# Two-layer adaLN transformer on one core: rows and sorts of the last experts given out earlier, their gathers made riders, their sums a part later

## The chip, the cores and the metric

The kernel runs on one core of one Trainium2 chip. The metric is the device time of one launch in microseconds (us), the median of several runs. Besides it there is one profiled execution; its trace gives every instruction's start and length on the engines: PE (TensorE matmul), PEld (TensorE weight load), DVE (VectorE), ACT (ScalarE), POOL (GpSimd) and SP (SyncE, which only issues DMAs here).

## The reference

Two transformer layers on x of shape (4, 1024, 256), all in float32. Each layer adds a gated attention and then a gated mixture of experts; c gives shift, scale and gate of each by a small product.

```python
h = _layernorm(x) * (1 + ca) + sa
x = x + ga * _L0_attn_ref(h, ...)      # causal softmax attention, 16 heads
h = _layernorm(x) * (1 + cb) + sb
x = x + gb * _L0_ffn_ref(h, ...)       # 16 experts, two products with GELU, best 2 of 16 per row
h = _layernorm(x) * (1 + ca) + sa      # second layer, its own c and weights
x = x + ga * _L1_attn_ref(h, ...)      # linear attention: cubed, normalised q and k
h = _layernorm(x) * (1 + cb) + sb
x = x + gb * _L1_ffn_ref(h, ...)       # the last experts, below

def _L1_ffn_ref(x, router_w, router_b, expert_w, expert_b):   # 8 experts, E = 8
    probs = jax.nn.softmax(xt @ router_w + router_b, axis=-1)
    gate, idx = jnp.max(probs, axis=-1), jnp.argmax(probs, axis=-1)
    out_all = jnp.einsum('th,ehd->ted', xt, expert_w) + expert_b[None, :, :]
    return gate[:, None] * jnp.take_along_axis(out_all, idx[:, None, None], axis=1)[:, 0, :]
```

So each of the 4096 rows goes to one of the eight last experts, the one with the largest router value.

## The kernel before, in words

x of the four batches stays in SBUF (`k.x[b]`, 128 rows x 8 tiles x 256). Four stages follow one another: attention 0, experts 0, attention 1, experts 1; the tail of each overlaps the head of the next. The change concerns the last two.

**Who sets the order.** The program text emits instructions; the tile framework reorders what does not depend on each other, except that instructions given to `k.pin` keep their order of emission on their engine. Each engine then runs its own queue in order. Text from different stages is interleaved by `Around`: a list of *tasks* (generators that are stepped one after the other, each `yield` worth some pieces) and a list of *riders* (generators of DMAs; only the first in the list is stepped). `around.step(pieces, rides)` advances both; the loop of attention 1 and that of the last experts call it at every step. An indirect DMA (`scatter`, `gather`) waits in addition for `k.anchor`, the matmul emitted last before it, so that these DMAs are spread over the stage.

**Attention 1** (`attention1`) runs over five rounds b = 0 to 4: `front(b)` (layer norm, transposes `ps_lnT` L153, products `ps_k` L1511, `ps_kv` L1502, `ps_q` L1537) beside `back(b - 1)` (`ps_o` L1574 with `on` L1580 on VectorE, transposes `ps_oT` L1589, a convolution along the rows into `y` L1597 and L1601, the projection `ps_pr` L1609, added to x at L1614). One step is taken of each in turn, and `pace[b] / 6` pieces of the tasks with each round of steps. When both are finished, `after_batch(b - 1)` gives out the tasks for the experts of that batch:

- `rows(b)`: layer norm statistics of the new x, then `routed_rows`: in two halves q of four tiles, `h` (L1030 on ScalarE; for batches 0 and 1 scaled and shifted by VectorE at L1045 and L1046) is stored to DRAM as `rows_in` (L1048), transposed (`ps_lnT` L1057) to `hT` (L1063, L1068), multiplied with the router (`ps_route` L794), turned (L799) and turned back (`ps_logits` L802).
- `sort(p)` for each of the three parts `PARTS = ((0, 1), (2,), (3,))` of batches: softmax, then the place of each row in an order by expert: two products `ps_rank` (L895), a chain of small VectorE operations, `index` (L933) and `ps_expert` (L949) with `offset` (L950). At its end it adds the rider `send(p)`, which reads the rows (`hs<-rows_in`, L1870) and scatters them (L964) to DRAM, sorted by expert.

**The last experts** (`Experts1.run`) work on tiles of 128 sorted rows, in 25 pairs of tiles: 11 of part 0, 7 of part 1, 7 of part 2. A pair: `xs<-sorted` (L1008, loads run up to five pairs ahead), transposes `ps_xT` (L1923) to `xT` (ScalarE, L1927 or L1930), and one pair later the product `ps_y` (L1938) with the expert's weights, found at a column that TensorE and VectorE load into a register from `offset` (L955); VectorE adds the bias (L1944) and for parts 1 and 2 multiplies the gate (L1946), and SP stores the pair (`results<-y`, L1947). While part p is not sent, the loop steps the tasks and riders; after each pair it takes `step(2, 2)`.

After a part's last pair comes the task `combine(p)`: for each of its row tiles a gather `ys<-results` (L974, issued by POOL, four ahead of its use, six buffers) and then a weighting by the router's probability: for part 0 `out` on ScalarE (L2002), gate and sum on VectorE (L2007, L2008), for parts 1 and 2 one VectorE operation (L1996). Every four tiles `out_dram<-x` is stored (L2010). After part 1, `count_sums` counts sums within bounds (12 VectorE operations, L495 to L498); after part 2, `out_of_bounds` turns the counts into a flag on which a general version of the whole, not run here, is taken or left.

Of the kernel before, what the change touches and what calls it, by code (L numbers as in the profile page):

```python
# [8 lines left out]
F32 = mybir.dt.float32  # L9
I32 = mybir.dt.int32  # L10
AF = mybir.ActivationFunctionType
ALU = mybir.AluOpType
# [479 lines left out]
def count_within(k, good, recs, low, high, count):  # L492

    nc = k.nc
    k.pin(nc.vector.tensor_scalar(good, recs, low, None, ALU.is_ge))  # L495
    nc.vector.tensor_scalar(recs, recs, high, None, ALU.is_le)
    nc.vector.tensor_tensor(good, good, recs, ALU.mult)
    nc.vector.tensor_reduce(count, good, AX.X, ALU.add)  # L498


def count_sums(k, pool):

    recs = [k.recs.rearrange("p n i j -> p (n i j)")]
    recs += [k.recs1[:, i].rearrange("p b t h -> p (b t h)") for i in range(2)]
    inverse = 1.0 / SUM_HI, 1.0 / SUM_LO
    for i, (rec, (low, high)) in enumerate(zip(recs, (inverse, (SUM_LO, SUM_HI), inverse))):
        good = pool.tile([P, 8 * B * H], F32, tag="xs", name="good", bufs=6)
        count_within(k, good, rec, low, high, k.good[:, i : i + 1])


def out_of_bounds(k, pool, psum):
# [505 lines left out]
def routed_rows(k, work, b, statistics, scale, shift, wr, br, ne, logits, scalar):  # L1017
# [31 lines left out]
        return h  # L1049

    h = yield from normalised(0)
    for q in range(2):
        hT = work.tile([P, CC, 512], F32, tag="hT", name="hT", bufs=1)
        for cc in range(CC):
            ps = k.misc.tile([P, 512], F32, tag="m", name="ps_lnT")
            for i in range(4):
                tr = nc.tensor.transpose(  # L1057
                    ps[:, i * P : (i + 1) * P], h[:, i, cc * P : (cc + 1) * P], k.ident
                )
                if i == 0:  # L1060
                    k.pin(tr)
            if scale is None:
                nc.scalar.activation(  # L1063
                    hT[:, cc], ps, AF.Identity,
                    bias=k.modF[:, cc, b : b + 1], scale=k.modF[:, 2 + cc, b : b + 1],
                )
            else:
                nc.scalar.copy(hT[:, cc], ps)  # L1068
            if q == 0 and cc == CC - 1:
                h = yield from normalised(1)  # L1070
            else:
                yield 1
        yield from route_logits(k, hT, wr, br, ne, work, logits[:, 4 * q : 4 * q + 4])
# [371 lines left out]
def attention1(ctx, k, a, after_batch=lambda b: None):  # L1445
# [172 lines left out]
    for b in range(B + 1):  # L1618
        while b == HB and k.awaited in k.around.tasks:
            k.around.step()  # L1620
        todo = ([front(b)] if b < B else []) + ([back(b - 1)] if b else [])
        pace = (6, 8, 6, 6, 12)[b]
        n = 0
        while todo:
            todo = [g for g in todo if next(g, k) is not k]
            n += pace
            k.around.step(n // 6)
            n %= 6
        if b:
            after_batch(b - 1)  # L1630


def attention1_general(ctx, k, a):
# [150 lines left out]
class Experts1:  # L1784


    def __init__(self, k, a, out):
# [16 lines left out]
        whole = Sorting(k, rt, E1, 1, NT * len(PARTS[0]))  # L1804
        fewer = whole.of_fewer(rt, NT)
        self.sortings = [whole if len(p) > 1 else fewer for p in PARTS]
        self.sent = set()

    def load_weights(self):
        k, a, nc = self.k, self.a, self.k.nc  # L1810
# [52 lines left out]
    def send(self, p, index):  # L1863
# [16 lines left out]
                yield  # L1880
        self.sent.add(p)

    def run(self, early):

        k = self.k
        nc = k.nc
        work = self.back = self.stack.enter_context(
            k.tc.tile_pool(name="f1_work", bufs=2, reuse_waits="tile")
        )
        ps_x = self.stack.enter_context(  # L1890
            k.tc.tile_pool(name="f1_ps_x", bufs=4, space=PSUM, reuse_waits="tile")
        )
        ps_o = self.stack.enter_context(
            k.tc.tile_pool(name="f1_ps_o", bufs=4, space=PSUM, reuse_waits="tile")
        )
        k.misc = ps_x

        pairs = [
            (p, list(range(g, min(g + 2, s.tiles))))
            for p, s in enumerate(self.sortings)  # L1900
            for g in range(0, s.tiles, 2)
        ]
        coming = []

        def fetch(n):

            for p, tiles in pairs[n + len(coming) : n + 5]:
                if p not in self.sent:
                    break
                xs = work.tile([P, 2, C], F32, tag="xs", name="xs", bufs=6)  # L1910
                k.sorted1[p].load(xs[:, : len(tiles)], tiles)
                coming.append(xs)

        def tiles_of(p, tiles, xs):

            n = len(tiles)
            at = self.sortings[p].offsets(
                self.state[p][1], tiles, [mybir.EngineType.PE, mybir.EngineType.DVE]
            )
            ps = ps_x.tile([P, 2, CC, P], F32, tag="m", name="ps_xT")  # L1920
            for j in range(n):
                for cc in range(CC):
                    nc.tensor.transpose(ps[:, j, cc], xs[:, j, cc * P : (cc + 1) * P], k.ident)  # L1923
            xT = work.tile([P, 2, CC, P], F32, tag="xT", name="xT", bufs=3)
            b = PARTS[p][0] if len(PARTS[p]) == 1 else None
            if b is None:
                nc.scalar.copy(xT[:, :n], ps[:, :n])  # L1927
            else:
                for cc in range(CC):
                    nc.scalar.activation(  # L1930
                        xT[:, :n, cc], ps[:, :n, cc], AF.Identity,
                        bias=k.modF[:, cc, b : b + 1], scale=k.modF[:, 2 + cc, b : b + 1],
                    )
            yield
            po = ps_o.tile([P, 2, C], F32, tag="o", name="ps_y")
            for j in range(n):
                for cc in range(CC):
                    k.anchor = nc.tensor.matmul(  # L1938
                        po[:, j], lhsT=xT[:, j, cc], rhs=self.we[:, cc, bass.ds(at[j], C)],
                        start=cc == 0, stop=cc == CC - 1,  # L1940
                    ).ins
            y = work.tile([P, 2, C], F32, tag="y", name="y", bufs=3)
            for j in range(n):
                nc.vector.tensor_tensor(y[:, j], po[:, j], self.be[:, bass.ds(at[j], C)], ALU.add)  # L1944
            if b is not None:
                nc.vector.tensor_tensor(y[:, :n], y[:, :n], bcast(self.gate[:, b], 1, n), ALU.mult)  # L1946
            nc.sync.dma_start(k.results1[p].part(tiles), y[:, :n])  # L1947

        again, before = None, None
        for n, (p, tiles) in enumerate(pairs):  # L1950
            if p not in self.sent and before is not None:
                next(before, None)
                before = None
            while p not in self.sent:
                k.around.step(1, 2)
            fetch(n)
            now = tiles_of(p, tiles, coming.pop(0))
            next(now)
            if before is not None:
                next(before, None)  # L1960
            before = now
            if n + 1 == len(pairs) or pairs[n + 1][0] != p:
                next(before, None)
                before = None
                if early and p + 2 == len(PARTS):
                    count_sums(k, work)
                if early and p + 1 == len(PARTS):
                    again = out_of_bounds(k, work, ps_x)
                k.around.tasks.append(self.combine(p))
            k.around.step(2, 2)  # L1970
        k.around.drain()
        self.stack.close()
        return again

    def combine(self, p):
        k, work = self.k, self.back
        nc = k.nc
        index, _, part = self.state[p]
        most = self.sortings[p].nt

        def fetch(n):
            ys = work.tile([P, C], F32, tag="ys", name="ys", bufs=6)
            self.sortings[p].gather(ys, k.results1[p], index[:, 0, n : n + 1])
            return ys

        coming = []
        for n in range(4):
            coming.append(fetch(n))
            yield 0.5
        for n in range(most):  # L1990
            j = n % 2
            b, t = PARTS[p][n // NT], n % NT
            ys = coming.pop(0)
            if len(PARTS[p]) == 1:
                xs = k.x[b][:, t]
                k.pin(nc.vector.scalar_tensor_tensor(  # L1996
# [2 lines left out]
            else:  # L1999
                if j == 0:  # L2000
                    y = work.tile([P, 2, C], F32, tag="out", name="out")
                k.pin(nc.scalar.activation(y[:, j], ys, AF.Identity, scale=part[:, n : n + 1]))  # L2002
            if n + 4 < most:
                coming.append(fetch(n + 4))
            if j == 1 and len(PARTS[p]) > 1:
                xs = k.x[b][:, t - 1 : t + 1]
                nc.vector.tensor_tensor(y, y, bcast(self.gate[:, b], 1, 2), ALU.mult)  # L2007
                nc.vector.tensor_tensor(xs, xs, y, ALU.add)  # L2008
            if t % 4 == 3:
                nc.sync.dma_start(  # L2010
# [176 lines left out]
```

## Time and profile before

| | us |
|---|---|
| median of 3 runs (lowest, highest) | 1087.03 (1085.85, 1088.48) |
| the profiled execution | 1087.63 |
| its span in the trace | 1085.8 |
| last `ps_pr` of attention 1 ends | 969.5 |
| last `ps_y` of the last experts ends | 1059.7 |
| last `y` of the last experts ends | 1062.15 |
| gathers (L974) of part 0, 1, 2 are issued at | 1010.8 to 1033.0, 1039.2 to 1050.3, 1065.1 to 1075.3 |

The span begins with the first instruction of the trace. A row of a window or group gives busy time; a wait is put down to the instruction that released the engine. A matmul in float32 appears twice in the trace's counts. Times from the trace are starts plus lengths, and two neighbouring instructions of an engine can overlap by some 0.1.

### The profile page before, as it was taken

The page shows a single profiled execution, that of the slowest core. Times are in us where ns is not written, and L with a number is a line of the kernel's source. Part 1 is how long each engine was busy: PE and PEld are TensorE (multiplying, and loading weights), DVE is VectorE, ACT ScalarE, POOL GpSimd, SP SyncE. Part 2 cuts the span into 40 slices and gives each one's busy share as a digit, 9 for nine tenths or more (in the row PEclk, how much of TensorE's full clock was granted, in tenths as well). Part 3 has the DMA queues.
Part 4 walks back from the last instruction along what each step waited for, and adds up shares of the span by engine and source line. Part 5 has one row for each costly group of instructions (what it writes and reads, how often), then busy time and mean ns, then how long its engine had stood idle before and what let it go on. Part 6 is the DMA issues. An engine that isn't in the chain of part 4 may idle for free.

```text
span 1085.8 us, 18090 instructions
## 1 busy us (share of the span) xinstructions
PE 945.7 (87%) x6072; PEld 559.8 (52%) x6072; DVE 620.4 (57%) x1987; ACT 602.5 (55%) x959; POOL 336.0 (31%) x528
## 2 busy tenths in 40 slices
PE   4899999999999999889679989986997989858760
PEld 2434434443443434335568878874464656547550
DVE  5822235422465155413676767993899968564572
ACT  0368655765477555775555657766654745523430
POOL 2013211311232234663004615612550100553632
PEclk9999999999999999999899999998999899989875
DMA  6995000100010001552825556624223201458764
GB/s 206 358 346 179 1 1 6 40 1 1 1 64 1 1 30 54 201 215 78 317 88 170 197 177 189 196 75 144 67 65 148 88 2 39 141 170 264 240 205 130
DMA packets 97142, 132.89 MB, mean 122 GB/s; under 512 B 8536, under 2 KB 84216, under 8 KB 96528
## 3 DMA queue, kind: packets, MB, share of 16 engines
q1 hardware_dynamic: 84656, 97.27, 26.9%
q0 software_dynamic: 11776, 33.57, 9.9%
q8 instruction: 52, 0.85, 0.3%
q10 hardware_dynamic: 608, 0.79, 0.3%
q14 instruction: 50, 0.41, 0.1%
HBM read 67.85 MB, written 63.75 MB: 121 GB/s over the span
## 4 chain that ended last, share of the span: by engine, by line
PE 63%; DVE 19%; issue 5%; DMA 5%; ACT 4%; POOL 1%; SPq 1%; DVEq 0%; ACTq 0%; POOLq 0%
PE ps_s L388 13%; PE ps_av L453 12%; PE ps_qk L364 6%; PE ps_y L1312 5%; PE ps_h L1247 4%; PE ps_v L349 3%; PE ps_out L427 3%; PE ps_pr L1609 3%; PE ps_y L1938 3%; PE ps_q L1537 2%; PE ps_k L1511 2%; DVE y L1601 2%; DMA ys<-results,index 2%; PE ps_lnT L1057 1%; DVE st L1258 1%
## 5 line engine op out<-in xcount | busy, mean ns | idle before, releaser
L396 ACT ACTIVATE pT<-ps_s 128x1024 f32<-128x1024 f32 x288 | 279.3, 1022 | 169.7 <-PE ps_s L388 167.2
L399 POOL TENSOR_SCALAR_AFFINE_SELECT pT<-pT 128x256 f32<-128x256 f32 x256 | 104.2, 431 | 328.4 <-ACT pT L396 323.7
L388 PE MATMUL ps_s<-qT,kT 32*128 32x512 f32 (+3 forms) x1536 | 178.8, 523 | 0.1
L453 PE MATMUL ps_av<-pT,v 128*32 128x512 f32 (+3 forms) x1536 | 165.2, 497 | 9.4 <-DVE turned L411 5.6
L964 POOL DMA_INDIRECT sorted<-hs,index x96 | 96.2, 1002 | 144.9 <-PE ps_y L1312 73.0
L974 POOL DMA_INDIRECT ys<-results,index x96 | 102.7, 1070 | 119.0 <-DMA results<-y 43.6
L388 PEld LDWEIGHTS ps_s<-qT,kT 32*128 32x128 f32 x1536 | 74.5, 185 | 95.5 <-issue 72.8
L453 PEld LDWEIGHTS ps_av<-pT,v 128*32 128x32 f32 x1536 | 40.6, 108 | 104.0 <-issue 58.7
L1247 PE MATMUL ps_h<-w,xT 128*128 x352 | 82.1, 386 | 6.5 <-DVE mv L1259 3.8
L1312 PE MATMUL ps_y<-w,act 128*128 x352 | 83.7, 392 | 4.2 <-DVE rs_seed L84 2.8
L411 DVE STREAM_TRANSPOSE turned<-ps_av 128x512 f32<-128x512 f32 x32 | 22.8, 712 | 98.9 <-PE ps_av L453 98.6
L1312 PEld LDWEIGHTS ps_y<-w,act 128*128 128x128 f32 x352 | 67.7, 197 | 14.0 <-ACT act L1295 4.8
L1247 PEld LDWEIGHTS ps_h<-w,xT 128*128 128x128 f32 x352 | 66.2, 193 | 15.9 <-issue 4.2
L1295 ACT ACTIVATE act<-ps_hT,gain 128x128 f32<-128x128 f32 x176 | 63.6, 463 | 16.9 <-PE ps_hT L1286 16.8
L1270 ACT ACTIVATE hid<-hid,nmr,rstd 128x256 f32<-128x256 f32 x88 | 47.5, 603 | 39.4 <-DVE nmr L1263 39.2
L1511 PE MATMUL ps_k<-wqkv,hT 128*128 128x512 f32 x128 | 61.9, 603 | 3.6 <-DMA wqkv<-in_wqkv_dram 2.8
L1938 PE MATMUL ps_y<-we,xT 128*128 x200 | 53.0, 412 | 10.6 <-ACT xT L1930 8.4
L371 DVE COPY qT<-ps_qk 128x512 f32<-128x512 f32 x16 | 11.0, 688 | 81.8 <-PE ps_qk L364 81.8
L103 DVE BATCH_NORM_STATS2 ln_st<-x 128x6 f32<-128x256 f32 x128 | 49.2, 407 | 0.5
L1255 DVE TENSOR_TENSOR hid<-ps_h,b 128x256 f32<-128x256 f32 x88 | 33.9, 415 | 26.6 <-PE ps_h L1247 21.5
L1938 PEld LDWEIGHTS ps_y<-we,xT 128*128 128x128 f32 x200 | 38.2, 204 | 20.1 <-ACT xT L1930 11.6
L374 DVE TENSOR_SCALAR kT<-ps_qk,par 128x512 f32<-128x512 f32 x32 | 22.5, 745 | 37.0 <-PE ps_qk L364 37.0
(223 smaller groups left out, 1499.4 us busy)
## 6 DMA issues: line engine op xcount, KB each, us to landing
xs<-sorted SPq DMA_DIRECT2D x69, 256.0 KB, 3.8
results<-y SPq DMA_DIRECT2D x69, 256.0 KB, 3.0
sorted<-zero SPq DMA_DIRECT2D x2, 6016.0 KB, 20.1
rows_in<-h SPq DMA_DIRECT2D x16, 512.0 KB, 2.9
hs<-rows_in POOLq DMA_DIRECT2D x32, 256.0 KB, 3.5
w<-in_w_dram SPq DMA_DIRECT2D x8, 1024.0 KB, 11.3
x<-in_x_dram SPq DMA_DIRECT2D x4, 1024.0 KB, 6.5
b<-in_b_dram SPq DMA_DIRECT2D x2, 2048.0 KB
```

Of the source, the lines that this page charges most:

```text
L364: nc.tensor.matmul(ps, lhsT=w[:, cc, g * P : (g + 1) * P], rhs=hT[:, cc, hf * 512 : (hf + 1) * 512], start=cc == 0, stop=cc == CC - 1,)
L388: k.anchor = nc.tensor.matmul(pair[hh // 2][:, hh % 2, c0 : c0 + w], lhsT=kTs[o][rows, kb * P : (kb + 1) * P], rhs=qT[rows, q1 - w : q1], ...
L396: nc.scalar.activation(pT, ps, AF.Exp, scale=1.0 / L**0.5)
L399: nc.gpsimd.affine_select(out=pT[:, :, c0 : c0 + P], in_=pT[:, :, c0 : c0 + P], compare_op=ALU.is_ge, fill=0.0, base=0, pattern=[[0, 2], [ ...
L453: nc.tensor.matmul(po[32 * hh : 32 * hh + 32, 512 - w :], lhsT=vs[b % 2][:, kb, 8 * g + 2 * hh + o, :], rhs=exps[b, g, o, u][hh // 2][:, h ...
L964: i = self.k.nc.gpsimd.indirect_dma_start(out=buffer.ap, out_offset=bass.IndirectOffsetOnAxis(ap=index, axis=0), in_=rows, in_offset=None, ...
L974: self.paced(self.k.nc.gpsimd.indirect_dma_start(out=rows, out_offset=None, in_=buffer.ap, in_offset=bass.IndirectOffsetOnAxis(ap=index, a ...
L1247: mm = nc.tensor.matmul(ph[:, j], lhsT=xTs[i // 2][:, j, cc], rhs=w1[:, cc, bass.ds(at[i + j], C)], start=cc == 0, stop=cc == CC - 1,)
L1295: o = nc.scalar.activation(act[:, j, cc], pt[:, j, cc], AF.Gelu, bias=gain[:, 1, cc, t : t + 1], scale=gain[:, 0, cc, t : t + 1],)
L1312: mm = nc.tensor.matmul(po[:, j], lhsT=acts[i // 2][:, j, cc], rhs=w2[:, cc, bass.ds(at[i + j], C)], start=cc == 0, stop=cc == CC - 1,)
L1511: k.anchor = nc.tensor.matmul(ps, lhsT=hT[:, cc, t * P : (t + 1) * P], rhs=wqkv[:, cc, C:], start=cc == 0, stop=cc == CC - 1,).ins
L1938: k.anchor = nc.tensor.matmul(po[:, j], lhsT=xT[:, j, cc], rhs=self.we[:, cc, bass.ds(at[j], C)], start=cc == 0, stop=cc == CC - 1,).ins
```

## The change

Five edits, all in attention 1 and the last experts:

1. `after_batch(b - 1)` is called as soon as `back(b - 1)` has ended, while `front(b)` still runs; the pace of round 3 goes from 6 to 8, and rounds 3 and 4 step two riders, not one.
2. For batches 2 and 3 (no scale given) both halves of `h` are made and stored ahead of the first transpose.
3. Gathers become riders of their own (`gathers(p)`), given out at a part's end; all 32 have 24 buffers. The sums come later: `combine(0)` is given out after part 1, `combine(1)` and `combine(2)` after the last pair. They no longer gather, but take what lies in `got`.
4. `count_sums` yields after each of its three arrays; one is counted after each of the pairs 7, 8 and 9 of part 0.
5. The step after a pair is 4 pieces, not 2, until the last part is sent. Transposes, `xT` and first products of a pair, and the gate of `combine`, are pinned.

The body of a pair moves from local functions to methods (`fetch`, `tiles_of`, `pair`, `products`) and is otherwise the same.

```diff
@@ routed_rows
     h = yield from normalised(0)
+    second = (yield from normalised(1)) if scale is None else None
...
             if q == 0 and cc == CC - 1:
-                h = yield from normalised(1)
+                if second is None:
+                    h = yield from normalised(1)
+                else:
+                    h = second
+                    yield 1
@@ attention1
-        todo = ([front(b)] if b < B else []) + ([back(b - 1)] if b else [])
-        pace = (6, 8, 6, 6, 12)[b]
+        behind = back(b - 1) if b else None
+        todo = ([front(b)] if b < B else []) + ([behind] if b else [])
+        pace = (6, 8, 6, 8, 12)[b]
         n = 0
         while todo:
             todo = [g for g in todo if next(g, k) is not k]
+            if behind is not None and behind not in todo:
+                behind = None
+                after_batch(b - 1)
             n += pace
-            k.around.step(n // 6)
+            k.around.step(n // 6, 1 + b // (B - 1))
             n %= 6
-        if b:
-            after_batch(b - 1)
@@ Experts1.run
-        again, before = None, None
-        for n, (p, tiles) in enumerate(pairs):
...
-            if n + 1 == len(pairs) or pairs[n + 1][0] != p:
-                next(before, None)
-                before = None
-                if early and p + 2 == len(PARTS):
-                    count_sums(k, work)
-                if early and p + 1 == len(PARTS):
-                    again = out_of_bounds(k, work, ps_x)
-                k.around.tasks.append(self.combine(p))
-            k.around.step(2, 2)
-        k.around.drain()
+        counts = count_sums(k, work) if early else iter(())
+        last = len(PARTS) - 1
+        while self.done < len(self.pairs):
+            p = self.pairs[self.done][0]
+            if p not in self.sent:
+                self.products()
+            while p not in self.sent:
+                around.step(1, 2)
+            self.pair()
+            if p == 0 and self.done > 6:
+                next(counts, None)
+            if self.done == len(self.pairs) or self.pairs[self.done][0] != p:
+                around.riders.append(self.gathers(p))
+                if p == last - 1:
+                    around.tasks.append(self.combine(0))
+            around.step(2 if last in self.sent else 4, 2)
+        for _ in counts:
+            pass
+        again = out_of_bounds(k, work, ps_x) if early else None
+        while around.riders:
+            around.step(0)
+        around.tasks += [self.combine(p) for p in range(1, last + 1)]
+        around.drain()
...
+    def gathers(self, p):
+        index = self.state[p][0]
+        for n in range(self.sortings[p].nt):
+            ys = self.back.tile([P, C], F32, tag="ys", name="ys", bufs=24)
+            self.sortings[p].gather(ys, self.k.results1[p], index[:, 0, n : n + 1])
+            self.got[p].append(ys)
+            yield
@@ combine
-            ys = coming.pop(0)
+            while not self.got[p]:
+                k.around.step(0)
+            ys = self.got[p].pop(0)
```

## The prediction

> **What bounds the kernel now.** I read the page's busy shares first, then the chain that ended last, then the stretch from 827 us to the end in windows, then the waits of each stage.
>
> ```profile
> PE 945.7 (87%) x6072; PEld 559.8 (52%) x6072; DVE 620.4 (57%) x1987; ACT 602.5 (55%) x959; POOL 336.0 (31%) x528
> ...
> PE 63%; DVE 19%; issue 5%; DMA 5%; ACT 4%; POOL 1%; SPq 1%; DVEq 0%; ACTq 0%; POOLq 0%
> ```
>
> TensorE bounds the whole (87%), but the change touches only what follows 827.7 us, and there the share is lower. The windows' columns are start:end, length, then busy us (and instructions) of PE, PEld, DVE, ACT, POOL, then granted clock, DMA share, GB/s:
>
> ```profile
> 827.00:842.00 15.00, 6.58 (x42) 4.96 (x40) 14.94 (x62) 4.50 (x9) 0.00 (x0) 0.86 0.64 245
> ...
> 866.00:885.00 19.00, 19.00 (x69) 10.39 (x67) 14.11 (x49) 8.63 (x17) 0.00 (x0) 1.00 0.01 1
> ...
> 916.00:937.00 21.00, 20.84 (x78) 11.54 (x77) 16.70 (x79) 10.80 (x21) 7.29 (x8) 1.00 0.13 44
> ...
> 951.00:960.50 9.50, 0.81 (x7) 0.63 (x6) 8.85 (x32) 3.17 (x5) 6.21 (x7) 0.65 0.37 112
> ...
> 997.00:1009.60 12.60, 12.40 (x66) 10.30 (x64) 3.87 (x10) 4.92 (x10) 7.33 (x8) 1.00 0.92 292
> ```
>
> The k and q phases (866 to 885, 916 to 937) leave TensorE no gap: small work put there by VectorE hides. At the seams between batches (827 to 842, 951 to 960) VectorE is full and TensorE stands. The waits of TensorE up to 970 us, then of all engines after it:
>
> ```profile
> PE ps_expert L949 <- DVE index L933: 7.7, 1, 7.7
> PE ps_lnT L1057 <- DVE ln_nmr L126: 5.7, 1, 5.7
> ...
> PE ps_lnT L1057 <- DVE h L1046: 3.6, 1, 3.6
> ...
> ACT out L2002 <- DMA ys<-results,index: 10.6, 8, 2.6
> ...
> PE ps_y L1938 <- ACT xT L1930: 8.4, 4, 3.6
> ...
> PE ps_xT L1923 <- DMA xs<-sorted: 6.4, 1, 6.4
> ```
>
> The last three are what the gathers cost now: ScalarE stands at `out` for a gathered row, the next pair's `xT` stands behind it, and TensorE behind that; and the part-3 loads of `xs` were issued only at 1043.34, behind results that VectorE's count of sums held up.
>
> **What the Trainium skill says.** "PSUM — Partial Sum Buffer", Engine vs sequencer instructions: ScalarE, VectorE and GpSimdE queues are strict FIFO and matmuls keep program order. The trace agrees (the 8.4 us above), and it is why the order of the queues decides here. "TensorE: Matmul & The Clock Gate", Part 1: an idle array falls back to a slower clock. The trace agrees: 0.65 in 951 to 960.5, and the 32 `ps_pr` that follow took 8.94 us at 0.80, against 7.9 in five pieces from 903 to 916. "Trainium Kernel Development and Optimization", Key Constraints: DMAs of SP, ACT and POOL share the same 16 engines. The trace agrees: 0.92 share at 292 GB/s while scatters, loads and results ran together; I take 300 GB/s (window 1000 to 1010) as full.
>
> **The change, part by part.** The order of each engine's instructions in the changed program is known; the durations are those of the trace of before.
>
> *1. Rows and sorts given out earlier (attention).* Same instructions, other places. I follow TensorE from 827.7 us, the end of batch 1's `ps_q`, where both programs are still alike.
> (a) Next in its order now stands `ps_lnT` of batch 0's rows, ahead of all 16 `ps_o` (before, these stood first and ran inside the gap). Its `h` needs VectorE: `out`, `x` 2.3, `qT` 0.6, ten interleaved statistics and the reciprocal root 3.5, then ScalarE's four `h` 2.1, then `h` scale and shift 2.4. That is 839.3: 11.6 us idle. Later waits in this seam, all for `h` or `hT`: 1.6+1.5+0.9+1.5+1.1. The four `y` (L1601, 1.2 each) end at 860.1 instead of 856.4, and `ps_pr` at 868.4 instead of 865.4 with one `ps_k` tile (1.7) fewer done: **+4.7**.
> (b) The k and q phase then takes in batch 1's rows (16 transposes 2.1, routing 1.2, logits 0.3 = 3.6); VectorE gets 4.5 of `h` scale and shift and would be near full (14.1 of 19 before), 1.3 lost: `ps_q` ends at 894.2 (before 884.6).
> (c) Here the first sort stands on TensorE's own path. Before, logits, rank and expert of sort 0 lay among `ps_k` and cost 0.2 of idle. Now between them are only four `ps_o` and one set of `ps_oT`. By the trace's sort (logits to sel 2.2 with `on` between, rank 0.5, count to past 3.5, semaphore steps of 0.4) `ps_expert` comes at 894.2+9.7; idle 0.6+1.5+2.9. Then `ps_o`, `on`, `ps_oT` to +14.1, `ps_lnT` to +15.6, a wait for ScalarE's `o`, `y`, `hT` to +17.5, three `ps_k` 5.2, `ps_pr` 7.4: 924.3. Before: 915.7, half a tile (0.9) behind and the sort's 0.8 not done. Now **+6.9**.
> (d) Batch 3's k and q: 5 tiles 8.6, `ps_kv` 3.7, `ps_q` 6.9, batch 2's rows 3.6, rest 0.2 = 23.0, plus 1.7 for `h` of batch 2 (eight in one block on ScalarE) and 1.5 for the k tiles behind it: 950.5.
> (e) Sort 1 ends at +5.1 (idle 1.2+3.4), no longer overlapped with the four `y`: `ps_o` and `ps_oT` to +12.6, then `o` 0.6, two `y` on ScalarE and four on VectorE to +19.3 (idle 6.7), `ps_pr` 8.9: 978.7. Before 969.5: **+9.2**. More idle means more time at a low clock: I add 1.3, so **+10.5**. Bounds: +4 if (b) to (d) lose nothing and half of (c) hides; +14 if the idle that I count (42 us against 27.8 in the trace) is simply added.
>
> *2. The last experts.* From the last `ps_pr` to the last `y` before: 1062.15-969.5 = 92.6. After it: rows of batch 3 and sort 2 come with only two pairs of tiles between them (before seven): x to `h` 4.1, eight `h` 4.2, `hT` 1.5, routing and logits 2.2, second half with a pair (1.9) 4.9, softmax 1.7, rank and sort 4.4 = 23.4 (before 26.4). Nine pairs of part 0 at 2.25 (the pace 997 to 1013) = 20.3; the count of sums (12 VectorE operations, 6.6 in the trace at 1036 to 1047) lies beside three of these, which need VectorE for only 1.3 each: nothing. Part 1, seven pairs: loads, results and two gathers are 0.77 MB a pair, 2.6 us at 300 GB/s; loads run ahead, so 2.4: 16.8. Part 2, seven pairs: VectorE bounds them: two `y` and gate 1.28, register load 0.54, and 8/7 of `out` and `x` 1.2 = 3.19: 22.3. Plus 0.7. Sum 83.5: **-9.1**. The 6.4 wait for `xs` goes (their loads no longer stand behind late results), the 10.6 of ScalarE goes (gathers are a part ahead); what is late next is VectorE in part 2. Bounds: -13 (part 1 at 2.25, VectorE's register load hidden) to -4 (landings of 6.5, the longest seen, hold up `y`, three buffers).
>
> *3. Tail.* Last `y` to end was 23.65, and its gathers, sums and stores are the same. New beside it: eight sums of part 1 (0.43 each, in the 5.8 that VectorE waited for the first gather) and 1.5 MB of `out_dram` among the eight gathers, 5 us of transfer at 300 GB/s in a time with 122 GB/s used: **+1.0** (0 to 2.5).
>
> *4. At nothing.* Moved memsets of `o` on POOL (0.1 each) stand among part 0's scatters, which end some 40 us before `y` of batch 3 reads `o`. On SP the two `rows_in` of batch 3 follow seven `xs` loads, as one did; the `gate_f` load moves behind a `rows_in`, and its reader is 100 us away. Gathers on POOL: 32 as before, 1.3 apart, behind the scatters. 24 `ys` buffers are in no trace; part 2's gathers reuse part 0's first eight, free a whole part before; 0, at worst 2.
>
> **Sum**: +10.5-9.1+1.0 = +2.4. The profiled execution took 1087.63 (span 1085.8), so 1090.0; the median of the three runs is 0.6 lower than it, so 1089.4.
>
> **Rivals.** *A, faster: the seams cost little.* The one mechanism is the sort in (c) and (e): if VectorE's small operations take the 0.15 that they show back to back, and `ps_o`, `ps_oT` fill the gaps, attention loses 4, the experts gain 12: -7, 1080. For it: VectorE has 5 us of slack per k phase. Against: 7.7 us at `ps_expert` in the trace of before. It wins if attention's loss is under 7. *B, slower: the stages' gain is eaten by transfers.* Part 1 at 0.92 DMA share, `y` held by landings: experts -4, attention +12, tail +1: 1096. For it: 292 GB/s already. Against: loads run five pairs ahead. *C, it does not do what it says:* gathers as riders are queued behind part 2's scatters, ready at 23.4 plus 10.4; part 0 ends at 43.7, so they are in time unless sort 2 slips by 10 us; then ScalarE waits as now, experts -5: 1093.5.
>
> **Numbers.** Some 0.2% (2.2 us) is what runs of this kernel can tell. The forecast, a near-cancellation, 0.40 (half of it, 0.20, within 0.2%, the rest slower); A 0.28; B 0.18; C 0.14. So faster 0.28, same 0.20, slower 0.52. Range 1080 to 1097: from A to B.
>
> **What would show it.** Last `ps_pr` near 980 rather than 969.5; a TensorE wait of 11 us at the rows' `ps_lnT` near 839 and 3 us at both `ps_expert`; no wait of `ps_xT` for `xs`, almost none of `out` for gathers; part 2 with VectorE full; last `y` to end near 24.6. It is wrong if the last `ps_pr` comes before 974, or if the time from there to the last `y` is over 88.

## The result, and the profile after

| | before | changed |
|---|---|---|
| median (lowest, highest), 11 runs each | 1086.97 (1083.31, 1088.48) | 1095.10 (1089.98, 1098.07) |
| the profiled execution, its span | 1087.63, 1085.8 | 1097.2, 1095.1 |

The ratio of the changed kernel to the one before is 1.0077, with a 95% interval of 1.0063 to 1.0091: some 8 us slower. A second measurement (fifth experiment) gave 1.0058 (1.0039 to 1.0077). The range held it and the side was right; the forecast of 1089.4 was 5.7 us too low.

The two traces are laid beside each other at marks that both have. They start at the end of batch 1's `ps_q`, up to which the programs are alike; the changed kernel's profiled execution was already 1.9 us later there (829.8 against 827.8), which is no work of the change.

| from, to | before | changed | difference | forecast |
|---|---|---|---|---|
| batch 1's `ps_q` to the last `ps_pr` (attention) | 141.7 | 147.9 | +6.2 | +10.5 |
| last `ps_pr` to the last `y` (experts) | 92.7 | 91.4 | -1.3 | -9.1 |
| last `y` to the end of the span (tail) | 23.6 | 26.0 | +2.4 | +1.0 |
| sum | 258.0 | 265.3 | +7.3 | +2.4 |

The page after, the lines of busy time. TensorE has the same 6072 instructions and is busy with them 4 us longer: the rest of the 9 us is waiting, at a lower mean clock (0.944 against 0.955).

```profile
span 1095.1 us, 18085 instructions
...
PE 949.8 (87%) x6072; PEld 562.9 (51%) x6072; DVE 623.0 (57%) x1987; ACT 601.3 (55%) x959; POOL 335.0 (31%) x528
```

Windows of the changed kernel at the places that the prediction showed for the kernel before (start:end, length, busy us and instructions of PE, PEld, DVE, ACT, POOL, granted clock, DMA share, GB/s): the seam behind batch 1's `ps_q`, batch 2's k and q phase, batch 3's, and the last seam.

```profile
829.80:841.50 11.70, 0.03 (x1) 0.06 (x1) 11.70 (x52) 3.44 (x7) 0.00 (x0) 0.65 0.70 269
869.10:893.40 24.30, 23.53 (x103) 12.86 (x103) 20.62 (x64) 14.62 (x29) 0.00 (x0) 1.00 0.11 40
923.80:947.80 24.00, 23.40 (x118) 12.56 (x116) 14.04 (x59) 14.71 (x30) 7.82 (x9) 1.00 0.58 190
953.00:967.80 14.80, 8.30 (x51) 7.01 (x49) 8.77 (x21) 4.42 (x6) 8.65 (x9) 0.85 0.20 71
```

TensorE does nothing for the first 11.7 us while VectorE is full, and in the two k and q phases it is nearly full (23.5 of 24.3, 23.4 of 24.0), with the rows of a batch now in each. The waits of TensorE in attention, from the changed kernel's list (line waited for, total, times, longest):

```profile
PE ps_lnT L1059 <- DVE ln_nmr L126: 11.7, 1, 11.7
PE ps_expert L950 <- DVE index L934: 6.5, 2, 3.7
PE ps_pr L1615 <- DVE y L1607: 6.1, 1, 6.1
```

And three waits of all engines from 975 us on; the last two were 10.6 and 8.4 before:

```profile
POOL ys L975 <- DMA xs<-sorted: 14.9, 1, 14.9
...
ACT out L2036 <- DMA ys<-results,index: 3.0, 2, 2.1
...
PE ps_y L1933 <- ACT xT L1925: 2.1, 3, 1.0
```

`out` waits 3.0 for gathers, `ps_y` 2.1 for `xT`, and `ps_xT` no longer waits for `xs`: the gathers as riders do what the change says. But the first gather comes at 1036.1, 14.9 after the last scatter, because part 0 ends at 1027.6 and no longer at 1005.2; its last results had landed at 1035.1 (the list names a load in their place).

That stage in windows, first of the kernel before, then of the changed one. The rows are: last `ps_pr` to the last sort's `ps_expert`; to the last `ps_y` of part 0; of part 1; of part 2; to the last `y`; to the first gather of part 2.

```profile
969.50:996.10 26.60, 21.41 (x141) 16.04 (x140) 13.67 (x65) 11.00 (x20) 8.93 (x11) 1.00 0.76 239
996.10:1005.20 9.10, 9.03 (x50) 7.81 (x51) 2.74 (x9) 2.35 (x4) 6.96 (x7) 1.00 0.88 281
1005.20:1030.80 25.60, 18.68 (x87) 14.77 (x86) 13.60 (x26) 12.34 (x26) 16.71 (x16) 0.90 0.76 236
1030.80:1059.70 28.90, 20.44 (x84) 15.92 (x82) 22.83 (x49) 8.64 (x19) 10.38 (x10) 0.80 0.63 198
1059.70:1062.20 2.50, 0.19 (x2) 0.11 (x2) 2.50 (x8) 0.00 (x0) 0.00 (x0) 1.00 0.88 295
1062.20:1065.10 2.90, 0.00 (x0) 0.00 (x0) 0.01 (x1) 0.00 (x0) 0.00 (x0) 0.66 0.64 206
```

```profile
977.70:1005.50 27.80, 14.30 (x85) 9.49 (x82) 10.23 (x55) 8.83 (x16) 2.95 (x4) 0.79 0.38 123
1005.50:1027.60 22.10, 21.53 (x108) 18.71 (x107) 10.63 (x26) 4.68 (x8) 7.90 (x8) 0.88 0.62 199
1027.60:1043.10 15.50, 15.44 (x86) 13.36 (x85) 10.60 (x24) 7.42 (x15) 5.54 (x5) 1.00 0.86 254
1043.10:1062.70 19.60, 16.60 (x87) 12.59 (x84) 16.71 (x32) 12.99 (x29) 15.29 (x15) 1.00 0.89 286
1062.70:1069.10 6.40, 0.07 (x2) 0.00 (x0) 4.87 (x11) 0.21 (x1) 4.65 (x5) 0.70 0.79 252
1069.10:1074.20 5.10, 0.00 (x0) 0.00 (x0) 4.42 (x10) 0.00 (x0) 0.00 (x0) 0.50 0.87 289
```

The reader is to compare the first two rows. Beside the sort the kernel before did seven pairs in 26.6 us, TensorE busy 21.4 at full clock; the changed kernel did two pairs in 27.8, busy 14.3 at 0.79. By these two rows a pair left there cost nothing; the five that were taken out are paid for in the second row, 22.1 instead of 9.1. From there parts 1 and 2 run 19.4 us faster than before (35.1 against 54.5): this is what gathers as riders, later sums and earlier counts bring together; no run takes them apart. The fifth row takes 3.9 of it back: after the last `ps_y` VectorE still has sums of part 0 to do.

### The profile page after: what moved, and what is told of

Read it like the earlier page. It is cut to its first block, busy times and chain, and to the rows that moved or that the text cites. A ratio compares the mean times of both kernels' runs of the same rounds, so it can differ in the third digit from the quotient of the medians.

```text
span 1095.1 us, 18085 instructions
## 1 busy us (share of the span) xinstructions
PE 949.8 (87%) x6072; PEld 562.9 (51%) x6072; DVE 623.0 (57%) x1987; ACT 601.3 (55%) x959; POOL 335.0 (31%) x528
## 3 DMA queue, kind: packets, MB, share of 16 engines
q1 hardware_dynamic: 84656, 97.27, 26.6%
## 5 line engine op out<-in xcount | busy, mean ns | idle before, releaser
L396 ACT ACTIVATE pT<-ps_s 128x1024 f32<-128x1024 f32 x288 | 279.3, 1021 | 169.8 <-PE ps_s L388 167.7
L453 PEld LDWEIGHTS ps_av<-pT,v 128*32 128x32 f32 x1536 | 40.7, 109 | 102.0 <-issue 59.7
L1327 DVE TENSOR_TENSOR y<-ps_y,b 128x256 f32<-128x256 f32 x88 | 35.1, 418 | 15.3 <-PE ps_y L1318 15.1
```

Of the source, the lines that this page charges most:

```text
L396: nc.scalar.activation(pT, ps, AF.Exp, scale=1.0 / L**0.5)
L453: nc.tensor.matmul(po[32 * hh : 32 * hh + 32, 512 - w :], lhsT=vs[b % 2][:, kb, 8 * g + 2 * hh + o, :], rhs=exps[b, g, o, u][hh // 2][:, h ...
```

## The experiments

My theory after the trace: attention loses 6 us at its seams; the experts' new order is worth some 9; and the pace of four pieces of side work a pair, which the diff has in `around.step(2 if last in self.sent else 4, 2)`, throws most of that away, as it leaves only two pairs beside a sort whose length is its own chain. The rival: the stage is bounded by VectorE and the gathers behind part 0, so that neither pace nor attention's delay matters there. Each series of kernels ran on one chip, twelve on a chip of its own, with runs of the kernel before beside it; ratios are to those. The columns of stages come from one traced execution of each kernel.

**First series.** *One: the loop of attention as before.*

```diff
-        behind = back(b - 1) if b else None
-        todo = ([front(b)] if b < B else []) + ([behind] if b else [])
-        pace = (6, 8, 6, 8, 12)[b]
+        todo = ([front(b)] if b < B else []) + ([back(b - 1)] if b else [])
+        pace = (6, 8, 6, 6, 12)[b]
...
-            if behind is not None and behind not in todo:
-                behind = None
-                after_batch(b - 1)
             n += pace
-            k.around.step(n // 6, 1 + b // (B - 1))
+            k.around.step(n // 6)
             n %= 6
+        if b:
+            after_batch(b - 1)
```

> The changed kernel with the loop of the last attention as it was before: rows and sorts are given out after a batch's front and back both end, pace 6 for batch 3, one ride a step. The experts' changes stay. Theory (the early rows and sorts lose 6 to 8 us in attention, and the changed experts about break even): last ps_pr near 970, then some 91 to the last y and 26 to the end as in the changed kernel, so about 1087.5 us, -1 to +2 against before. Rival (the experts' changes are the loss, attention's delay is made up behind it): still +5 to +8, 1092 to 1095.

*Two: the kernel before with the changed loop and both halves of `h` first.* The edit is the reverse of that, in the other kernel, and in `routed_rows`:

```diff
     h = yield from normalised(0)
+    second = (yield from normalised(1)) if scale is None else None
...
```

> The kernel before with the changed loop of the last attention (rows and sorts at the end of a batch's back part, pace 8, two rides in batch 3 and after, both halves of h first) and the experts as before. Theory: last ps_pr near 976, then 92.6 and 23.7 as before: about 1093 us, +5 to +8 against before. Rival (experts' changes are the loss): within 2 us of before, 1087 to 1089.

*Three: two pieces a pair.*

```diff
-            around.step(2 if last in self.sent else 4, 2)
+            around.step(2, 2)
```

> The changed kernel with one number changed: two pieces of the side work a pair of tiles throughout the last experts, instead of four until part 2 is sent. Theory (with four pieces only two pairs lie beside the last sort, TensorE falls to a granted clock of 0.79 there and part 0 ends 20 us late, so that 24 gathers run back to back): seven pairs come back into the sort's stretch, it stays about 26 to 28 us long, the gathers of part 0 start 10 to 20 us earlier, and the time falls by 6 to 12 us against the changed kernel: 1083 to 1089. Rival (VectorE in part 2 decides, it has the same work whenever part 0 ends): no faster than 1093.

*Four: one and three together.*

> Both of the former: attention's loop as before, and two pieces a pair throughout the last experts, with gathers as riders, sums a part later and checks early. Theory: the two gains add, last ps_pr near 970, 76 to 84 to the last y, 24 to 26 to the end: 1076 to 1082 us, faster than both kernels. Rival (VectorE in part 2): about 1086, no better than before.

| | ratio (95%) | attention | experts | tail |
|---|---|---|---|---|
| one | 1.0047 (1.0030, 1.0065) | 142.4 | 101.2 | 25.9 |
| two | 1.0059 (1.0038, 1.0079) | 149.4 | 96.9 | 24.1 |
| three | 1.0087 (1.0064, 1.0110) | 148.2 | 94.8 | 25.8 |
| four | 0.9987 (0.9969, 1.0004) | 144.2 | 89.6 | 26.2 |

The traced execution of three was 9 us faster than its median, those of one and two 6 and 7 slower, so their columns are rough.

Two came as the theory had it: the changed loop, with both halves of `h` first and the experts as before, loses 0.59%, 6.5 us. One and three did not: one lost 5 us where 0.5 was expected, three gained nothing. Four against one says that the pace is worth 0.6%, three (1.0087, beside the 1.0077 of the changed kernel in the first result) seems to say that it is worth nothing. But this chip was another case: the kernel before took 1097.2 us on it (1086.8 and 1087.9 in the next two series), and the traces hold waits that the other chips' do not show. Experiment one between parts 1 and 2:

```profile
ACT xT L1923 <- remote: 14.5, 1, 14.5
...
PE ps_y L1931 <- issue: 12.7, 1, 12.7
DVE y L1940 <- remote: 7.4, 2, 5.3
```

"Remote" stands where the semaphore that ended a wait was raised with no instruction ending near it. Here TensorE's transposes are on record at 1045, but ScalarE, which waited for them, started at 1058, and TensorE stood for 12.7 us. Such rows lie in all four of these traces between 950 and 1064, and in none of the traces of the other chips. So the stage times of this series are not to be compared with those of the first traces, and the pace was tried again. Why three gained nothing here stays open.

**Second series.** *Five: the changed kernel unaltered.*

> The changed kernel unaltered, beside the next three, so that they have a control of the same runs. Theory and rival alike: +7 to +9 us against before, ratio 1.006 to 1.009. If it is well off that, differences of less than 3 us among the former four kernels, which ran without it, are not to be read.

*Six: the rows of batch 0 late.*

```diff
                 behind = None
-                after_batch(b - 1)
+                if b > 1:
+                    after_batch(b - 1)
...
+        if b == 1:
+            after_batch(0)
```

> The changed kernel, but the rows of batch 0 are given out at the end of the loop for batch 1, as before; those of batches 1 and 2 and both sorts stay early. Theory (TensorE's wait of 11.7 us at the rows' ps_lnT near 840 is a large part of what attention loses): that wait goes, and 3 to 5 us of the loss with it: ratio to before 1.003 to 1.005. Rival (the loss sits at the two sorts on TensorE's path, and slack behind the first seam would have taken the wait up): within 1.5 us of the changed kernel.

*Seven: the kernel of three again.*

> The changed kernel with two pieces of side work a pair throughout the last experts, as in the third experiment, now beside the changed kernel itself. Theory (four pieces leave only two pairs beside the last sort, at a low clock, and that is why the stage saved 1 us where 9 were forecast): 4 to 10 us faster than the changed kernel. Rival (the stage is bounded by what comes after part 0, VectorE in part 2 and the pace of 1.3 us a gather): within 2 us of it, as the third experiment hinted.

*Eight: of four, with the sums begun early.*

```diff
-                if p == last - 1:
-                    around.tasks.append(self.combine(0))
+            if self.done == sum(q < last - 1 for q, _ in self.pairs) + 3:
+                around.tasks += [self.combine(0), self.combine(1)]
...
-        around.tasks += [self.combine(p) for p in range(1, last + 1)]
+        around.tasks.append(self.combine(last))
```

> A version meant to be faster than both: attention's loop as before, the experts as changed with two pieces a pair, and the sums of parts 0 and 1 begun after the third pair of part 1 rather than at its end, so that VectorE has eleven pairs to lay them beside in place of seven, and the eight sums of part 1 are done before the tail. Theory (VectorE in part 2 and the stores of part 1 in the tail set the end): 3 to 7 us under the kernel without it, so 0.991 to 0.996 of before. Rival (gathers arrive no sooner, so sums begun earlier wait for them on VectorE's or ScalarE's queue with the pairs behind): no gain or +2 to +5 us against before.

| | ratio (95%) | attention | experts | tail |
|---|---|---|---|---|
| five, changed | 1.0058 (1.0039, 1.0077) | 148.0 | 89.9 | 26.2 |
| six, rows 0 late | 1.0037 (1.0024, 1.0051) | 144.6 | 90.7 | 26.4 |
| seven, pace 2 | 1.0001 (0.9990, 1.0012) | 148.3 | 83.9 | 25.8 |
| eight, sums early | 1.0014 (1.0000, 1.0029) | 144.1 | 90.2 | 25.9 |

Seven settles the pace: 0.57% between it and five, intervals apart, 6 us, all of it in the experts' column, and the whole change then costs nothing against the kernel before. Its windows, rows as above:

```profile
975.10:1003.60 28.50, 19.97 (x120) 15.09 (x118) 12.57 (x60) 10.70 (x19) 2.95 (x4) 0.88 0.52 166
1003.60:1018.70 15.10, 14.47 (x70) 12.46 (x71) 9.44 (x22) 2.93 (x5) 7.95 (x8) 0.89 0.69 215
1018.70:1034.50 15.80, 15.38 (x86) 13.40 (x85) 10.41 (x23) 7.82 (x16) 7.96 (x9) 1.00 0.92 284
1034.50:1052.40 17.90, 16.52 (x86) 12.77 (x84) 15.33 (x29) 11.85 (x27) 13.94 (x14) 1.00 0.89 277
1052.40:1059.00 6.60, 0.09 (x2) 0.00 (x0) 5.33 (x13) 0.73 (x2) 3.99 (x4) 0.76 0.79 254
1059.00:1063.70 4.70, 0.00 (x0) 0.00 (x0) 4.45 (x10) 0.00 (x0) 0.00 (x0) 0.50 0.75 254
```

Five pairs lie beside the sort now, and the first row is 28.5 us, against 27.8 with two. The stretch of the sort is not made shorter by fewer pairs: 26.6 with seven (before), 28.5 with five, 27.8 with two. The second row falls from 22.1 to 15.1. The rival is out: the last `y` comes as much earlier as part 0 ends earlier.

Six takes the wait at `ps_lnT` from 11.7 to 5.7, as in the kernel before, and 3.4 us out of attention's 6.3 (in the trace; the two ratios' intervals overlap). Eight was its rival's, 1.0014 where four, the kernel without early sums, had 0.9987 on the chip of the first series: begun three pairs into part 1, the sums come to ScalarE before their gathers. From its waits between 1018 and 1046:

```profile
ACT out L2034 <- DMA ys<-results,index: 12.1, 7, 4.0
...
PE ps_y L1931 <- ACT xT L1923: 5.7, 2, 4.4
```

That is the wait that the change had removed (10.6 and 8.4 before), brought back. This traced execution was 4.5 us over eight's median, so its 90.2 for the experts is too long to stand for the kernel.

**Third series.** *Nine: six and seven together.*

> The changed kernel with both single cures together: the rows of batch 0 given out as before, and two pieces a pair throughout the last experts. Theory (the two costs lie in different stages and add): attention 144 to 145 us from the end of batch 1's ps_q to the last ps_pr (before 141.7, changed 148), 84 from there to the last y (before 92.7, changed 90 to 91), 26 for the tail (before 23.6): 2 to 4 us under before, ratio 0.996 to 0.998. Rival (a gain in attention is given back in the experts, since scatters and gathers come no earlier): within 1 us of before.

*Ten: of nine, batch 1's rows and sort 0 late too.*

```diff
-                if b > 1:
+                if b > 2:
                     after_batch(b - 1)
...
-        if b == 1:
-            after_batch(0)
+        if 0 < b < 3:
+            after_batch(b - 1)
```

> As the former, and rows of batch 1 with sort 0 also given out as before; only rows of batch 2 with sort 1 stay early. Theory (a sort on TensorE's own path costs some 2 to 3 us at each seam, as the forecast had for sort 0): attention 142 to 143, the rest as in the former: 3 to 6 us under before, ratio 0.9945 to 0.997. Rival (rows of batch 1 and sort 0 then crowd the front of batch 3 together with rows of batch 2 and sort 1): no better than the former, or worse.

*Eleven: of ten, the sums of part 0 two pairs earlier.*

```diff
-                if p == last - 1:
-                    around.tasks.append(self.combine(0))
+            if self.done == sum(q < last for q, _ in self.pairs) - 2:
+                around.tasks.append(self.combine(0))
```

> As the former, with the sums of part 0 begun two pairs before the end of part 1 instead of at its end. Theory (after the last ps_y VectorE still has sums of part 0 before the last y, and the 0.5 MB stores of these sums lie between the last results and the first gather of part 2, 4.7 to 5.3 us after the last y against 3.0 before): last y 2 to 3 us earlier and first gather 1 us nearer to it, 2 to 4 us under the former. Rival (part 0's gathers, 1.3 us apart on GpSimd, have not landed and ScalarE's out holds up xT, as in the version with sums begun earlier still): no gain, or a loss of 2 to 4 us.

| | ratio (95%) | attention | experts | tail |
|---|---|---|---|---|
| nine | 0.9965 (0.9950, 0.9979) | 144.4 | 83.9 | 25.9 |
| ten | 1.0008 (0.9988, 1.0028) | 147.5 | 84.0 | 26.4 |
| eleven | 1.0001 (0.9986, 1.0015) | 147.9 | 84.1 | 26.1 |

Nine is faster than both kernels, by 0.35% against the one before and about 1% against the changed one; the two cures add, stage by stage. Nine and seven differ by the late rows of batch 0 alone, and their intervals are apart, though on two chips: the cure that six left unsettled is there by the runs too. Ten is a miss, and its rival came: with batch 1's rows and sort 0 late again attention is 3 us longer. Among its TensorE waits between 820 and 972 are these two:

```profile
PE ps_lnT L1059 <- DVE h L1047: 4.3, 1, 4.3
...
PE ps_rank L896 <- DVE part L1872: 2.6, 1, 2.6
```

Nine has no such `ps_lnT` row there, and 0.8 where `ps_rank` of sort 1 waits 2.6: batch 1's rows now crowd into batch 3's round with batch 2's, and sort 1 comes later in it. With sort 1 early, sort 0 costs less early than late. Eleven: no gain, the rival again. `out` waits 8.0 for gathers (none in seven, which begins the sums at the end of part 1) and the last `y` comes no sooner: it follows the last `ps_y` by 3.9 us where ten had 6.3, but that `ps_y` comes later by as much.

*Twelve: of nine, without part 0's stores to the output.*

```diff
-            if t % 4 == 3:
+            if t % 4 == 3 and p:
```

> The version with rows of batch 0 given out as before and two pieces a pair, leaving out the four stores of part 0's sums to the output (512 KB each): batches 0 and 1 of the output are not written. It measures what these stores cost late. Theory (they hold up the landing of the last results, so that the first gather of part 2 comes 5 us after the last y where it came 3.0 us after it before): the gap falls from 5.2 to about 3, the tail from 25.9 to about 23.7; part 2 may gain another 1 or 2 from freer DMA engines; in all 2 to 4 us under the version with the stores (0.9965 of before), so 0.993 to 0.995. Rival (the gap is the gathers' own: GpSimd and the landing of the last results, whatever else moves): gap and tail stay within 0.5 us, ratio 0.996 to 0.997.

It gave 0.9962 (0.9944 to 0.9979), no different from nine by the runs. In the one trace, that of the fastest of its eight executions, attention took 144.8, the experts 81.3 and the tail 24.3; last `y` to first gather stayed 4.9 (5.2 in nine), where 3 was expected. So these stores do not hold up the first gather. Windows of twelve, from the last `ps_y` to the last `y`, and to the first gather:

```profile
1047.00:1052.40 5.40, 0.06 (x2) 0.00 (x0) 4.71 (x11) 0.17 (x1) 4.18 (x5) 0.95 0.61 176
1052.40:1057.30 4.90, 0.00 (x0) 0.00 (x0) 4.58 (x11) 0.00 (x0) 0.93 (x2) 0.50 0.64 203
```

The experts' 2.6 us lie in part 2. From part 1's last `y` to the last `y`, first nine, then twelve:

```profile
1034.10:1056.80 22.70, 15.39 (x78) 11.78 (x76) 19.19 (x37) 11.60 (x26) 16.33 (x16) 0.93 0.87 271
1031.90:1052.40 20.50, 14.66 (x78) 12.05 (x76) 19.01 (x38) 11.66 (x27) 15.93 (x16) 0.99 0.70 212
```

VectorE has the same work in both, 19 us, and a DMA share of 0.70 in place of 0.87 goes with 2.2 us less. So VectorE is not all that holds part 2; the two ratios neither show this gain nor exclude it.

## Why the prediction came out as it did

**Step 1, attention: right in kind, 4 us too large.** The waits are where it put them: 11.7 at `ps_lnT` (11.6), 2.8 and 3.7 at the two `ps_expert` (2.9 and 3.4), 6.1 at `ps_pr` for `y` (6.7). From batch 1's `ps_q`, its marks were 40.7 for batch 1's `ps_pr`, 66.5 for the next `ps_q`, 96.6, 122.8 and 151.0, plus 1.3 for the clock; measured 39.3, 63.6, 94.0, 118.0 and 147.9. So (a) was 1.4 too long, (b) 1.5, (d) 2.2; (c) was right within 0.3, and the last part was 1.7 longer than (e) said, more than its 1.3 for the clock. The terms listed in (a) add up to 10.9 and not 11.6; `wg` (L1566, 0.7), which VectorE does among them, is not in the list. Ten shows what the sum could not: the early sort 0 that (c) charges is cheaper than the late one once sort 1 is early.

**Step 2, the experts: the step that failed.** It gave 83.5, with a bound of 4 us of gain at least; 91.4 was measured, over the 88 that the text named as its own limit. Term by term: the sort's stretch 23.4 against 27.8, nine pairs of part 0 20.3 against 22.1, part 1 16.8 against 15.5, part 2 with its 0.7 23.0 against 26.0.

The first term is the root (its listed terms add up to 23.0). I put two pairs beside the sort, charged one of them, 1.9 in the second half of the rows, and took 3 us off the stretch. That pair's `ps_y` took 1.99. The other pair stood between the routing and the logits of the first half, for which the sum had 2.2 with no pair in it; from the end of `hT` at 987.1 to the logits at 993.7 it was 6.6. TensorE's own order there, in the changed kernel, and the clock:

```profile
988.08 1.09 PE L1916 MATMUL ps_xT<-ident,xs 128*128 128x128 f32 x4 [0.97 <-issue]
989.10 0.66 PE L795 MATMUL ps_route<-hT,wr 128*32 128x128 f32 x8
989.68 3.78 PE L1933 MATMUL ps_y<-we,xT 128*128 x8
993.26 0.42 PE L803 MATMUL ps_logits<-ident,turned 128*128 128x128 f32 x1
...
997.08 1.99 PE L1933 MATMUL ps_y<-we,xT 128*128 x8
```

```profile
983.40:993.60 10.20, 7.91 (x36) 5.25 (x37) 0.39 (x2) 4.26 (x8) 2.95 (x4) 0.50 0.68 230
```

So a pair that the sum left out stood in the chain, and at half the clock: of the 4.4 missed some 1.8 are the slow clock (3.78 against 1.99), an estimate from these two lines, and the rest for the most part the pair itself. Five, the same kernel run again, shows the same 3.78 and 1.99. The Trainium skill, "TensorE: Matmul & The Clock Gate", Part 1, says that an idle array falls back to a slower clock, and I used it for attention's `ps_pr` and not here; the trace agrees: TensorE had stood from 978.2 to 982.4, and the kernel before, with seven pairs in the stretch, kept 1.00.

Nine pairs at 2.25 then began cold as well (0.88). Part 2 was for the most part VectorE's, as predicted (7 pairs at about 3.2 from the last `y` of part 1, 1046.5, to 1069.1, with VectorE busy for 19.2 of the 22.6), but not full, which the trace of twelve puts in part on DMA traffic. It also began late, with part 1's last `y` 3.4 us behind its `ps_y`.

That seven measures 83.9 and the sum said 83.5 is chance, not a proof of its terms: there the sort took 28.5 and the six remaining pairs 15.1.

**Step 3, the tail: +2.4 for +1.0**, just within its bound of 2.5. The eight sums of part 1 lie in the gap as said and cost nothing. What grew is the gap itself, last `y` to first gather 2.9 before and 5.1 now; first gather to end is 20.7 and 20.9. The last `results` store landed later: in the semaphore counts of the trace, 14 of its 16 parts were in by 1071.6 and the last at 1073.3; before, all sixteen came within 0.2 of each other. Twelve excludes part 0's stores as the cause. The Trainium skill, "DMA: Bandwidth & Descriptors", Latency and other measured facts, says that two of the sixteen DMA engines, 7 and 15, are usually slower than the others in traces, and puts that, as a guess, on the descriptor rings of GpSimd's DMAs. The last gather of part 1 was issued at 1067.6 in the changed kernel, 1.5 us ahead of the last `results` store, and 13 us ahead of it in the one before, which would fit that. But in all twelve traces with the changed experts the last part came 1.4 to 2.3 us after the fourteenth, in experiment one too, where that gather was 8.9 us ahead; in the two with the experts as before it came within 0.1. So nearness to a gather does not explain it by itself, and no run here shows which engines were late. It stays open.

**Step 4, at nothing:** right as far as the traces go; no wait for a `ys` buffer appears.

**The total** is in the range partly by luck: attention cost 4.3 us less than forecast, the experts 7.8 and the tail 1.4 more. With attention as forecast it would have been near 1099, above the 1097 of the range.

**The rivals.** A (cheap seams) was to win if attention lost under 7: it lost 6.2 and A did not win, because the experts gained 1.3 and not 12. B named the right total, 1096, for reasons that did not occur: attention lost 6 and not 12, and part 1 ran faster than forecast at a DMA share of 0.86. C did not occur: the scatters of part 2 were out by 1021, before part 0 ended. None had a pace in it. The loss that decided was the five pairs taken from beside the sort. The prediction charged them in part 0 and took 3 us back from the sort: 43.7 for the first two rows together, where 35.7 stood before. Measured, they took 49.9.

## What to carry to other kernels

A latency chain on the critical path is the place to put throughput work: how long the chain takes must be measured with and without that work, and not be made shorter on paper by taking it out. Of the work that stays, each piece must be given its place in the chain, and the clock that it will find there. When several edits come together, look for the one scalar among them that paces two queues against each other; here a 4 in place of a 2 cost 6 us, as much as the early rows and sorts did. And what is begun earlier must be asked for its inputs: sums begun before their gathers put back the very wait that riders had taken away.

## What was not expected of the hardware

On one chip of those used, engines stood for work that by the records was long done: up to 14.5 us at one wait, some rows in each of four traces, and the kernel before ran 1% longer there. On the others the traces show no such row. These traces also lack records of semaphores (in experiment one TensorE's count is raised 998 times, 1058 in the fifth), so what held the engines is not shown. A result that turns on a few us in such a stage needs its control on the same chip. Of the last store of 256 KB in the changed kernel, the last of sixteen parts came 1.6 us after the fourteenth.
